# Sums over keys in a cross attention: one moving column against the weights, or ones as weights in four column groups with a block transpose on VectorE

## The chip, the core and the metric

The kernel runs on one core of a Trainium2 chip. The time is device microseconds of one execution. A core has TensorE (PE; its weight loads are shown apart, as PEld), VectorE (DVE), ScalarE (ACT), GpSimd (POOL) and the queues that start DMAs (SP among them). Matrix products go from SBUF through TensorE into PSUM, which has banks of 512 float32 columns in 128 partitions.

## What is computed

A decoder of two layers, float32, batch 4, 256 tokens of 256 features. The first layer has a self attention of 16 heads, a cross attention over 1601 context tokens and a feed-forward part with ternary weights. The second has a recurrence, a cross attention (the one changed here), and a mixture of eight experts. Cut to what matters, the second cross attention is, for each batch `b` and each of its 16 heads of width 128, in four groups that share keys and values:

```
q = rope(rmsnorm(LN(x) @ Wq))                  # 256 queries a head
k = rope(rmsnorm(concat(LN(x), ctx) @ Wk))     # 256 + 1601 = 1857 keys, one set for 4 heads
v = concat(LN(x), ctx) @ Wv
e = exp(q @ k.T / sqrt(128) - max)             # softmax over the keys
x = x + ((e @ v) / sum(e, over keys)) @ Wo
```

The kernel scales by folding factors into the keys, so the form is the same. The changed lines compute `1 / sum(e, over keys)`.

## The kernel before

The first part of the run, to about 560 us, takes the four batches through the first layer and the recurrence. From there to the end the second cross attention and the experts run interleaved.

The attention goes by pairs of heads (class `Pair`, 32 pairs: 4 batches, 4 groups, 2 pairs each). A pair has 2 x 256 = 512 queries, which are the free dimension of all its tiles; keys lie on the partitions, in 15 chunks of 128 (the last has 65). A pair passes through these stages:

- `score` (L1309): two score tiles bsc a step on TensorE (128 keys x 512 queries). ScalarE copies each to SBUF with the key's factor (L1310), VectorE keeps a running maximum acc (L1312, L1314).
- `maximum`: four transposes of acc (tm, L1321), a maximum on VectorE (mq, L1323), and four transposes that spread it over the partitions (bc, L1327).
- `exponential`: VectorE subtracts (L1331), ScalarE takes the exponential (L1334), and GpSimd adds the chunks up into one tile `sum` of 128 x 512 (L1337, L1346). Of the very last pair, VectorE adds the last chunks into a second tile `rest` (L1340, L1343).
- `weigh` (L1355): values times exponentials, summed over the chunks in one PSUM bank, bpo.
- `finish`: ScalarE copies bpo to aT (L1361). What is left in `sum` is the sum over 128 partitions, for each of the 512 queries. Line 1368 takes it: for each block of 128 queries a matmul with that block of `sum` as the stationary weights and one column of ones as the moving operand, which leaves the sums with the queries on partitions, one column for a block (ts, 128 x 4). VectorE takes the reciprocal (rs, L1373). Then aT is projected with the output weights (bpw, L1381, two matmuls for a head), and VectorE multiplies by rs and adds into x (L1385).

A matmul of float32 is carried out in two passes and each pass is a record of its own in the profile; each pass has its weight load.

Between the stages stand the preparations of the next group: projections and rotations of keys (pk, L1238; ropek, L1156; tpk, L1249; kTb, L1251) and queries (pq, L1199; ropeq; rnq, L1159; L1163; tpq, L1211), and the experts of the batch before (mph, L1013; it, L1018 to L1020; mpe, L1026; x, L1031). GpSimd adds the two halves of a rotation (L1156) and takes the power for the norm (L1159) in the same queue in which it sums the exponentials.

The order around the change is written out by hand: `steps` has one step for two key chunks, `put` gives the pieces of other work places between them, and a pair's `finish` is cut in four pieces by its yields, so that the sums, the two halves of the projection and the additions lie some steps apart. A scheduler then may move an instruction past neighbours on its engine. PSUM tiles such as bsc, tm, ts, pk and bpw come in turn from a ring of six banks (`p1`); a bank comes free when its last reader is done. Tiles of `sm` are small SBUF tiles with a given number of buffers.

Of the kernel before, what the change touches and what calls it, by code (L numbers as in the profile page):

```python
# [20 lines left out]
P = 128  # L21
# [94 lines left out]
def decoder_kernel(ctx: ExitStack, tc: tile.TileContext, at, t, out):  # L116
    nc = tc.nc
    V, A, G, T = nc.vector, nc.scalar, nc.gpsimd, nc.tensor
# [18 lines left out]
    def p1(name):  # L137

        ring[0] += 1
        if psb and ring[0] % 3 == 0:  # L140
            return psb[0].tile([P, 512], F32, tag="one", name=name, bufs=2)
        return psa.tile([P, 512], F32, tag="one", name=name, bufs=4)
# [17 lines left out]
    def fa(b, name, dt=F32):  # L160

        return fr.tile([P, 512], dt, tag=f"a{b}", name=name, bufs=NA)
# [9 lines left out]
    def sm(shape, tag, name, bufs=2, dt=F32):  # L172
        return small.tile(shape, dt, tag=tag, name=name, bufs=bufs)
# [30 lines left out]
    def cc(name):  # L204
        o, n = at[name]
        return cst[:, o : o + n]
# [1078 lines left out]
    class Pair:  # L1285
# [71 lines left out]
        def finish(self):  # L1357
            b, g, nm = self.b, self.g, self.nm
            e, su = gt[b, g], self.sum
            aT = fa(1, f"aT{nm}")  # L1360
            A.copy(aT, self.po)  # L1361
            yield

            ts = p1(f"ts{nm}")
            parts = (su, self.rest) if self.final else (su,)
            for i in range(4):
                for a in parts:
                    T.matmul(
                        ts[:, i : i + 1], lhsT=a[:, i * P : (i + 1) * P], rhs=cc("ones")[:, 0:1],
                        start=a is parts[0], stop=a is parts[-1],  # L1370
                    )
            rs = sm([P, 4], "rs", f"rs{nm}")
            V.reciprocal(rs, ts[:, 0:4])  # L1373
            if not self.final:
                yield

            for h in range(2):
                pw = p1(f"bpw{nm}{h}")
                for j in range(2):
                    o = h * 256 + j * P  # L1380
                    T.matmul(  # L1381
                        pw[:, j * 256 : j * 256 + 256], lhsT=aT[:, o : o + P], rhs=e["wo"][:, self.h + h, :], start=True, stop=True
                    )
                for j in range(2):
                    V.scalar_tensor_tensor(  # L1385
                        xs[b][:, j, :], pw[:, j * 256 : j * 256 + 256], rs[:, 2 * h + j : 2 * h + j + 1], xs[b][:, j, :], ALU.mult, ALU.add
                    )
                if not self.final:
                    yield
# [222 lines left out]
```

## Time and profile before

| what | value |
|---|---|
| time, median of 3 runs | 1772.86 us (1772.27 to 1773.15) |
| profiled execution, its own time | 1771.45 us |
| its span, first to last instruction | 1769.6 us |
| mean granted TensorE clock | 0.988 |
| sums (ts, L1368): matmul passes / weight loads | 264 / 264 |
| reciprocals (rs, L1373) | 32, median 173 ns |
| GpSimd adding into `sum` (L1346) | 411, 533.4 us |

A row of a group names line, engine, operation, output and inputs, their sizes, then the count and the durations. Durations of matmuls overlap, since TensorE starts a pass before the last one has left; the distance from start to start tells what a pass costs. In the chain of work that ended last each piece is what held up the next one; an engine that is not on it had time to spare there. The numbers around a duration in a wait name the instruction that ended it.

### The profile page before, as it was taken

To read this page: it belongs to the slowest core of one execution; us is meant where nothing else is said; L and a number is where in the kernel's file an instruction comes from. 1 tells how busy PE (TensorE), PEld (TensorE's weight loads), DVE (VectorE), ACT (ScalarE), POOL (GpSimd) and SP (SyncE) were. 2 spreads that over 40 slices of the span, in tenths; PEclk is the share of its full clock that TensorE was granted. 3 is DMA by queue.
4 is the path that set the end of the run, shared out by engine and by line. 5 is a ranking of instruction groups with operands and counts; after the bars stand their busy time and mean duration, and the time that the engine had idled before them with its cause. 6 is when DMAs were issued, how large, how long until landed. Compare 5 with 4: busy or idle time off the path is not lost.

```text
span 1769.6 us, 20922 instructions
## 1 busy us (share of the span) xinstructions
PE 1712.0 (97%) x6792; PEld 1017.1 (57%) x6792; DVE 1299.4 (73%) x2420; ACT 994.3 (56%) x1741; POOL 866.6 (49%) x719
## 2 busy tenths in 40 slices
PE   7989989988999999999999999999999999999998
PEld 4555668765555555455555656555565555555557
DVE  5662476789658777797787788788778778777775
ACT  2456653655556656567565555656555556655551
POOL 2210023212116677666776565676666656666460
PEclk9999999999999999999999999999999999999999
DMA  6321234201231011121211212121121203111102
GB/s 235 106 94 54 86 100 128 72 1 59 69 122 57 28 60 51 37 80 36 60 41 60 70 42 81 48 88 41 60 55 57 75 31 111 31 51 46 54 1 66
DMA packets 106565, 116.91 MB, mean 66 GB/s; under 512 B 9664, under 2 KB 80468, under 8 KB 106456
## 3 DMA queue, kind: packets, MB, share of 16 engines
q1 hardware_dynamic: 105160, 114.02, 20.9%
q10 hardware_dynamic: 1296, 1.54, 0.3%
q8 instruction: 55, 0.90, 0.2%
q14 instruction: 54, 0.44, 0.1%
HBM read 101.38 MB, written 14.16 MB: 65 GB/s over the span
## 4 chain that ended last, share of the span: by engine, by line
PE 75%; DVE 8%; ACT 7%; POOL 6%; issue 2%; DMA 1%; ACTq 0%; POOLq 0%; DVEq 0%
PE bpo L1355 19%; PE bsc L1309 19%; PE pk L1238 7%; PE vah L347 4%; POOL sum L1346 3%; PE bpw L1381 3%; PE mph L1013 3%; ACT s L1334 2%; PE pq L1199 2%; PE xsc L655 2%; ACT s L1310 2%; PE xpo L700 1%; PE mpe L1026 1%; PE sc L536 1%; PE tpk L1249 1%
## 5 line engine op out<-in xcount | busy, mean ns | idle before, releaser
L1346 POOL TENSOR_TENSOR sum<-sum,s 128x512 f32<-128x512 f32 (+1 forms) x411 | 533.4, 1298 | 84.8 <-ACT s L1334 59.0
L1309 PE MATMUL bsc<-qTb,kTb 128*128 128x512 f32 (+1 forms) x960 | 457.7, 597 | 2.4 <-ACT kTb L1251 2.3
L1355 PE MATMUL bpo<-s,vb 128*128 128x512 f32 (+1 forms) x960 | 458.7, 596 | 0.0
L1310 ACT ACTIVATE s<-bsc,kn 128x512 f32<-128x512 f32 (+1 forms) x480 | 317.4, 684 | 232.8 <-PE bsc L1309 217.8
L1314 DVE SCALAR_TENSOR_TENSOR acc<-bsc,kn,acc 128x512 f32<-128x512 f32 x448 | 333.8, 745 | 104.0 <-ACT s L1310 89.3
L1331 DVE TENSOR_TENSOR s<-s,bc 128x1024 f32<-128x1024 f32 (+1 forms) x256 | 289.5, 1143 | 15.2 <-PE bc L1327 15.1
L1334 ACT ACTIVATE s<-s 128x1024 f32<-128x1024 f32 (+1 forms) x256 | 256.4, 1006 | 52.3 <-DVE s L1331 50.7
L1309 PEld LDWEIGHTS bsc<-qTb,kTb 128*128 128x128 f32 (+1 forms) x960 | 174.2, 187 | 186.5 <-issue 135.2
L1355 PEld LDWEIGHTS bpo<-s,vb 128*128 128x128 f32 (+1 forms) x960 | 169.1, 191 | 131.9 <-issue 129.6
L1156 POOL TENSOR_TENSOR ropek<-ropek,ropuk 128x512 f32<-128x512 f32 (+1 forms) x64 | 77.0, 1203 | 182.3 <-DVE ropuk L1151 181.3
L1337 POOL TENSOR_TENSOR sum<-s 128x512 f32<-128x512 f32 x32 | 40.9, 1277 | 187.1 <-ACT s L1334 187.1
L1238 PEld LDWEIGHTS pk<-wkv,cTk 128*128 128x128 f32 x832 | 101.6, 192 | 9.2 <-issue 4.5
L1163 ACT ACTIVATE ropeq<-ropeq,rnq 128x128 f32<-128x128 f32 x128 | 41.2, 390 | 112.6 <-POOL rnq L1159 109.0
L1238 PE MATMUL pk<-wkv,cTk 128*128 128x128 f32 x832 | 103.3, 275 | 0.0
L347 PE MATMUL vah<-wv,vcT 128*128 128x512 f32 (+1 forms) x156 | 80.0, 651 | 4.9 <-DMA vcT<-in_ctxT 2.9
L1312 DVE TENSOR_SCALAR acc<-bsc,kn 128x512 f32<-128x512 f32 x32 | 24.0, 750 | 64.2 <-ACT s L1310 64.2
L1381 PEld LDWEIGHTS bpw<-wo,aT 128*128 128x128 f32 x256 | 49.7, 194 | 34.7 <-issue 23.0
L1159 POOL TENSOR_TENSOR kn<-ssk,nhalf 128x4 f32<-128x4 f32 (+1 forms) x64 | 64.9, 1015 | 8.9 <-DVE ssk L1158 8.9
L1156 POOL TENSOR_TENSOR ropeq<-ropeq,ropuq 128x512 f32<-128x512 f32 x32 | 43.8, 1369 | 47.5 <-ACT s L1310 35.5
L1381 PE MATMUL bpw<-wo,aT 128*128 128x256 f32 x256 | 67.0, 386 | 0.0
L350 ACT COPY vst<-vah 128x512 f32<-128x512 f32 (+1 forms) x52 | 30.3, 590 | 63.0 <-PE vah L347 30.2
L268 POOL TENSOR_TENSOR rsr_xa<-rse_xa,nhalf 128x2 f32<-128x2 f32 x4 | 3.4, 853 | 126.0 <-DVE rse_xa L266 126.0
(500 smaller groups left out, 2592.2 us busy)
## 6 DMA issues: line engine op xcount, KB each, us to landing
cTk<-in_ctxT SPq DMA_DIRECT2D x32, 512.0 KB
v<-vst SPq DMA_DIRECT2D x48, 256.0 KB
vb<-v SPq DMA_DIRECT2D x48, 256.0 KB
wq<-in_wq SPq DMA_DIRECT2D x16, 512.0 KB
wo<-in_wo SPq DMA_DIRECT2D x16, 512.0 KB
wi<-in_wi SPq DMA_DIRECT2D x32, 256.0 KB
vcT<-in_ctxT SPq DMA_DIRECT2D x12, 512.0 KB
xcT<-in_ctxT SPq DMA_DIRECT2D x12, 512.0 KB
```

What stands on the lines that cost most here:

```text
L347: T.matmul(pv[0:r, :], lhsT=cT[:, c, k * P : k * P + r], rhs=wv[c], start=c == 0, stop=c == 1)
L1156: G.tensor_tensor(r4, r4, u4[:, :, ::-1, :], ALU.add)
L1159: G.tensor_tensor(rn, ss[:, 0:n], nhalf[:, 0:n], ALU.pow)
L1238: T.matmul(pk[:, q, 0:w], lhsT=src, rhs=e["wkv"][:, c, 0:w], start=c == 0, stop=c == 1)
L1309: T.matmul(pc[0:n, :], lhsT=e["kT"][:, k * P : k * P + n], rhs=q, start=True, stop=True)
L1310: A.activation(s[0:n, i, :], pc[0:n, :], AF.Copy, scale=e["kn"][0:n, k : k + 1])
L1314: V.scalar_tensor_tensor(self.acc[0:n, :], pc[0:n, :], e["kn"][0:n, k : k + 1], self.acc[0:n, :], ALU.mult, ALU.max)
L1331: V.tensor_tensor(s[0:n, 0:w, :], s[0:n, 0:w, :], self.bc[0:n, None, :].to_broadcast([n, w, 512]), ALU.subtract)
L1334: A.activation(s[0:n, 0:w, :], s[0:n, 0:w, :], AF.Exp)
L1346: G.tensor_tensor(self.sum[0:n, :], self.sum[0:n, :], s[0:n, i, :], ALU.add)
L1355: T.matmul(self.po, lhsT=e["v"][0:n, k, :], rhs=self.s[c][0:n, i, :], start=k == 0, stop=k == NCH - 1)
L1381: T.matmul(pw[:, j * 256 : j * 256 + 256], lhsT=aT[:, o : o + P], rhs=e["wo"][:, self.h + h, :], start=True, stop=True)
```

## The change

The four matmuls of a pair's sums change sides. Before, a block of `sum` (128 x 128) is the weights and one column of ones moves. After, 32 columns of ones are the weights, and 128 columns of `sum` move: query number 32 i to 32 i + 31 of each of the four blocks, so the moving operand is read in four runs of 32 columns. Matmul i writes the 32 PSUM partitions from 32 i; all 32 hold the same sums, for 128 queries. VectorE transposes the 128 x 128 result in blocks of 32 x 32 into a new SBUF tile `sq` with one buffer, after which the sum of query 128 k + p stands in partition p, column 32 k. The reciprocal reads these four columns from SBUF. For the last pair, the two parts are now the outer loop: four matmuls of `sum`, then four of `rest`.

```diff
             ts = p1(f"ts{nm}")
             parts = (su, self.rest) if self.final else (su,)
-            for i in range(4):
-                for a in parts:
+            for a in parts:
+                for i in range(4):
                     T.matmul(
-                        ts[:, i : i + 1], lhsT=a[:, i * P : (i + 1) * P], rhs=cc("ones")[:, 0:1],
+                        ts[32 * i : 32 * i + 32, 0:P], lhsT=cc("ones")[:, 0:32],
+                        rhs=a.rearrange("p (k q) -> p k q", k=4)[:, :, 32 * i : 32 * i + 32],
                         start=a is parts[0], stop=a is parts[-1],
                     )
+            sq = sm([P, P], "sq", f"sq{nm}", 1)
+            V.transpose(sq, ts[:, 0:P])
             rs = sm([P, 4], "rs", f"rs{nm}")
-            V.reciprocal(rs, ts[:, 0:4])
+            V.reciprocal(rs, sq.rearrange("p (k q) -> p k q", k=4)[:, :, 0])
```

In the built programs TensorE, GpSimd and the DMA queues keep the order of their instructions, apart from one bpo matmul in one place and, in the last pair, one of two matmuls of mph that follow the sums, which stands behind the projection bpw instead of ahead of it. On VectorE a transpose stands where each reciprocal stood, and the reciprocal comes, in most pairs, one instruction later. A few instructions of VectorE and ScalarE that prepare the angles of a batch or take exponentials change places with neighbours.

## The prediction

> **What bounds the kernel now.** I read the page's first part, then the chain that ended last, then the groups of the line that is changed.
>
> ```profile
> PE 1712.0 (97%) x6792; PEld 1017.1 (57%) x6792; DVE 1299.4 (73%) x2420; ACT 994.3 (56%) x1741; POOL 866.6 (49%) x719
> PE 75%; DVE 8%; ACT 7%; POOL 6%; issue 2%; DMA 1%; ACTq 0%; POOLq 0%; DVEq 0%
> L1368 PEld LDWEIGHTS ts<-cst,sum x256: 188/192/193, 580.2 to 1729.6; 128*128 128x128 f32 x128
> L1368 PE MATMUL ts<-cst,sum x256: 166/250/251, 580.7 to 1729.7; 128*128 128x1 f32 x128
> L1373 DVE RECIPROCAL rs<-ts x32: 161/173/183, 586.2 to 1730.2; 128x4 f32<-128x4 f32 x32
> ```
>
> TensorE is busy for 97% of the span and carries 75% of the chain, so time taken out of its stream counts where the chain runs through that stream. The sums (L1368) are 128 matmuls with one moving column each, plus 8 more for the last pair's `rest`; every one is split in two passes (256 and 16 records), and each pass loads its own 128x128 weights. Stretched out in time for TensorE, one group of sums looks like this (start, duration of the whole group, number of passes):
>
> ```profile
> 579.80 1.02 PE L1309 MATMUL bsc<-qTb,kTb 128*128 128x512 f32 x2
> 580.66 0.95 PE L1368 MATMUL ts<-cst,sum 128*128 128x1 f32 x8
> 581.47 1.96 PE L1355 MATMUL bpo<-s,vb 128*128 128x512 f32 x4
> 583.27 0.59 PE L1309 MATMUL bsc<-qTb,kTb 128*128 128x512 f32 x1
> ```
>
> A pass of 512 columns takes 0.43 us of the stream: the two scores (bsc) start at 579.80 and the sums at 580.66. The eight passes of the sums hold the stream until 581.47, 0.81 us, or 0.10 us each, for one column apiece. The four bpo passes then need 583.27 - 581.47 = 1.80 us, where four times 0.43 is 1.72: the second bpo weight load was queued behind the sums' loads. One group of sums therefore costs 0.81 + 0.08 = 0.89 us, and all single groups stand between the same kind of neighbours and repeat this to some hundredths.
>
> **The change, on TensorE.** It removes the eight passes that each load 128 weight columns and puts in four matmuls (eight passes) with 32 weight columns and 128 moving columns, each into its own 32 output partitions. The trace before has this form: the self attention weighs its values (L571, L574) in four groups of 32 columns. One such place, TensorE alone:
>
> ```profile
> 97.39 1.98 PE L347 MATMUL vah<-wv,vcT 128*128 128x512 f32 x4 [0.63 <-ACT pT L557]
> 99.30 0.64 PE L571 MATMUL po<-pT,values 128*32 128x256 f32 x8
> 99.76 0.40 PE L574 MATMUL po<-sm,values 128*32 128x128 f32 x8
> 100.09 1.78 PE L446 MATMUL pq<-wqkv,xqkv 128*128 128x256 f32 x7
> ```
>
> L571's eight passes of 256 columns hold the stream for 99.76 - 99.30 = 0.46 us. At 0.43/512 us a column one pass is 0.215, so eight in a row would be 1.72 us: four run at once, in two sets. L574's passes, which have the 128 columns of the new ones, go from 99.76 to 100.09, 0.33 us: two sets of 0.11 are 0.22, and 0.11 more lies ahead of the next matmul of full width. Ahead of 99.30 the last of the four vah passes ended at about 97.39 + 4 x 0.43 = 99.11 to 99.2 (the first was late by its weights), a gap of 0.09. Sum of the new group: 0.09 to get into the narrow form, 0.03 for the first narrow weights (L571's first set takes 0.46 - 0.215 = 0.245), 2 x 0.11 for the sets, 0.11 to get out, and 0.11 for the next 128 weight columns, which can't be loaded ahead: 0.56 us. Against 0.89 one group saves 0.33 us.
>
> The last pair has two parts: 16 passes before, 1728.30 to 1730.01 = 1.71 plus 0.08; after, four sets instead of two, 0.56 + 0.22 = 0.78. It saves 1.0. The order of the built instructions also moves one of two matmuls of mph (L1013) there from ahead of bpw to behind it: bpw comes 0.43 sooner, and mph has slack, since the products (`it`) wait on VectorE anyway.
>
> A rule speaks against this. The Trainium skill, page "TensorEngine Tiling (Array Packing)", section "Instruction Overhead", gives a matmul a floor of about 60 cycles, so one moving column costs as much as 60; the page "TensorE: Matmul & The Clock Gate" puts the floor at about 25 ns. By that rule eight passes would be 0.2 us, the new group 0.36 us dearer, and the kernel about 20 x 0.36 = 7 us slower. The row decides: 0.10 us a pass, because each pass brings 128 new weight columns. I take the row.
>
> **What of it lies on the path.** The chain in order of time passes through a sum group in some pairs and beside it in others. Two stretches (start, us):
>
> ```profile
> 614.59 1.72 PE bsc L1309 x4
> 616.31 0.79 PE ts L1368 x8
> 617.10 1.82 PE bpo L1355 x4
> ...
> 580.42 1.23 POOL sum L1346
> 581.64 0.98 POOL rnq L1159
> 582.62 0.02 issue
> 582.65 1.28 ACT ropeq L1163 x4
> ...
> 588.11 0.33 ACT kTb L1251
> 588.44 0.04 issue
> 588.48 1.98 PE bsc L1309 x4
> ```
>
> At 616 the chain runs through the sums. At 580 it runs through GpSimd (rotation of q behind queued sums) and ScalarE, and TensorE waits at 588.48 whatever it did at 580.66: a faster group only makes that wait longer. Read through the whole chain, the groups at 616, 689, 767, 804, 839, 913, 993, 1076, 1117, 1155, 1230, 1309, 1350, 1389, 1469, 1543, 1622, 1662, 1694 and 1713 are on it, 20 in all, and the last double one; eleven are not. So 20 x 0.33 = 6.6, plus 1.0 + 0.43 at the end: 8.0 us. The eleven are costed at nothing: POOL and ACT hide them, and they would give 3.6 us more if that work came earlier too. Some of the 20 must have a second path close behind; I take off 1.0 us (three groups), an estimate.
>
> **The clock at the end.** The profile by windows (length, then busy time and count of PE, PEld, DVE, ACT, POOL, granted clock, DMA):
>
> ```profile
> 1727.20:1730.60 3.40, 3.40 (x22) 2.63 (x22) 1.20 (x2) 0.58 (x1) 0.47 (x1) 1.00 0.02 5
> 1730.60:1734.00 3.40, 3.40 (x10) 2.65 (x9) 0.79 (x2) 0.00 (x0) 0.00 (x0) 0.51 0.00 0
> ```
>
> Right behind the last sums the clock is 0.51, and the eight bpw passes start 0.43 us apart, where 0.215 is the pace of 256 columns. Seven gaps of 0.21 are 1.5 us on the chain. The two other half-clock stretches among the pairs (from 754 and 1062) follow waits of TensorE of 2.3 us and more, so I read this one as an answer to 1.7 us of one-column passes. With 0.8 us of full passes I expect it to go: 1.5 us, at worst nothing.
>
> **VectorE.** It gains 32 transposes of 128x128 from PSUM. No such row exists; the nearest, a product of 128x128 from PSUM (L1150), takes 0.28 us on average, the reciprocal of four columns 0.173. I take 0.28, with ends of 0.17 and 0.6 (should it run at half that pace). The reciprocal stays at 0.16 to 0.18. That is 32 x 0.28 = 9.0 us of VectorE, on an engine that is busy for 914 of the 1168 us from 560 to 1728. The transpose inherits the reciprocal's wait for the sums and its place; one other instruction stands between it and the reciprocal. Queued behind it are the running maxima (acc L1314) that free score buffers. In the place shown, the sums end at 581.6 and the reciprocal runs at 586.20, so the wait is long over, and its first user (x L1385) runs at 591.23. I cost it at nothing; idle time of VectorE hides it. Without that cover it is 21 x 0.28 = 5.9 us. GpSimd and the DMA queues keep their order; ScalarE moves a few instructions by two or three places.
>
> **Sum.** 8.0 - 1.0 + 1.5 = 8.5 us off the profiled execution's own 1771.45 us (span 1769.6 and 1.85 around it), 1762.95. The median of the runs shown is 1772.86, 1.4 above that execution; the same saving gives **1764.4**.
>
> **Rivals.**
> *Everything passes through* (chance 0.10). The eleven also give 3.6, nothing is taken off: 8.0 + 3.6 + 1.5 = 13.1, 1759.8. For it: what GpSimd waits for begins with TensorE's own scores. Against: those scores lie ahead of the sums in each of the eleven.
> *The gain is absorbed* (0.12). GpSimd's sums or VectorE's transposes become the late part in most pairs. VectorE at full price takes 5.9 of 8.5 and leaves 2.6: 1770.3, no measurable change. For it: 0.28 us against 0.33 saved, pair by pair; the waits for mq at 753, 1062 and 1376 come when VectorE or ScalarE is late. Against: 254 us of idle VectorE in that stretch.
> *The four groups don't run at once* (0.08): slower. The new moving operand is read in four runs of 32 columns, while L571's and L574's is contiguous; no row shows such a read. In series, eight passes of 0.11 make the group 0.09 + 0.03 + 0.88 + 0.11 + 0.11 = 1.22, 0.33 dearer than now; 20 x 0.33 + 0.3 = 6.9 slower, 1779.8. It decides from where a set of four takes over 0.275 us instead of 0.11.
>
> **How the numbers follow.** The forecast has 0.70, with its own range of 1761 to 1768 (clock and second paths either way). The range for 8 in 10 reaches to the case where everything passes and toward the absorbed one: 1759.5 to 1769.3. Under 0.2%, 3.5 us, no change can be told from none: faster 0.80, same 0.12, slower 0.08.
>
> **What would show it.** Right: the sums' passes start in sets of four, 0.11 us apart, and the stream is held 0.45 us, with 0.11 more at the next pass; the wait at 588 grows by 0.3; the half clock at 1730 is gone; transposes near 0.28 us with the reciprocal still long ahead of x. Wrong: narrow passes 0.1 us apart one by one; new waits of bsc or bc on DVE; VectorE's chain share up by more than 0.3 points.

## The result and the profile after

The changed kernel takes 1764.06 us (median of 6 runs, 1762.96 to 1767.17), the kernel before 1772.26 beside it (6 runs): a ratio of 0.9958, interval 0.9945 to 0.997. By the ratio it is faster by 0.42%, 7.4 us (the medians lie 8.2 apart). The forecast was 1764.4.

The page of the profile after, busy time and the chain:

```profile
PE 1697.8 (96%) x6792; PEld 986.5 (56%) x6792; DVE 1301.3 (74%) x2452; ACT 994.5 (56%) x1741; POOL 867.1 (49%) x719
PE 71%; DVE 9%; ACT 8%; POOL 7%; issue 3%; DMA 1%; POOLq 0%; ACTq 0%; DVEq 0%
```

TensorE is busy for 14 us less and the span is 7.1 shorter (1762.5 against 1769.6). From the first to the last sums it is busy for 9.6 us less (1128.3 against 1137.9) and the time is 4.5 shorter: about half of what TensorE saved stayed as time in which it waits. The groups of the sums, and one of them in time, TensorE alone:

```profile
L1369 PEld LDWEIGHTS ts<-sum,cst x256: 106/108/110, 581.1 to 1724.3; 128*32 128x32 f32 x128
L1369 PE MATMUL ts<-sum,cst x256: 272/285/298, 581.1 to 1724.4; 128*32 128x128 f32 x128
L1375 DVE STREAM_TRANSPOSE sq<-ts x32: 300/305/318, 586.5 to 1724.9; 128x128 f32<-128x128 f32 x32
L1377 DVE RECIPROCAL rs<-sq x32: 159/162/178, 587.4 to 1725.3; 128x4 f32<-128x4 f32 x32
```
```profile
580.14 1.02 PE L1309 MATMUL bsc<-qTb,kTb 128*128 128x512 f32 x2
581.10 0.42 PE L1369 MATMUL ts<-sum,cst 128*32 128x128 f32 x8
581.45 1.98 PE L1355 MATMUL bpo<-s,vb 128*128 128x512 f32 x4
583.27 1.02 PE L1309 MATMUL bsc<-qTb,kTb 128*128 128x512 f32 x2
```

From the start of the two scores to the first score behind bpo there are now 583.27 - 580.14 = 3.13 us, of which six passes of 0.428 are 2.57: the sums cost 0.56. In the kernel before it was 583.27 - 579.80 = 3.47, so 0.90. Taken from single starts, a group costs 0.559 us in 30 of the 32 pairs, against 0.899 before: 0.34 less in each.

For a reading by place I laid the start of each pair's sums beside the same start before. The stretch up to the first sums has no edit in it and differs by itself (0.43 us later here, between 1.7 earlier and 1.5 later in the other profiles). From the first to the last sums the time goes from 1147.64 to 1143.13 us, 4.51 less; from the last sums to the end (the tail) from 41.33 to 38.32, 3.01 less. Between two groups the time changes by -0.34 or by nothing, nearly in turn. Two pairs lose: pair 6 0.96, pair 12 0.29. The windows behind the last sums, with the columns of the prediction, have no half clock:

```profile
1723.20:1726.60 3.40, 3.40 (x27) 2.19 (x26) 1.67 (x4) 0.59 (x1) 0.43 (x1) 1.00 0.02 5
1726.60:1730.00 3.40, 2.02 (x10) 1.43 (x9) 3.24 (x11) 0.38 (x1) 0.00 (x0) 1.00 0.09 24
```

### The profile page after: what moved, and what is told of

It is laid out like the page before. It is cut to its first block, busy times and chain, and to the rows that moved or that the text cites. A ratio compares the mean times of both kernels' runs of the same rounds, so it can differ in the third digit from the quotient of the medians.

```text
span 1762.5 us, 20956 instructions
## 1 busy us (share of the span) xinstructions
PE 1697.8 (96%) x6792; PEld 986.5 (56%) x6792; DVE 1301.3 (74%) x2452; ACT 994.5 (56%) x1741; POOL 867.1 (49%) x719
## 4 chain that ended last, share of the span: by engine, by line
PE 71%; DVE 9%; ACT 8%; POOL 7%; issue 3%; DMA 1%; POOLq 0%; ACTq 0%; DVEq 0%
PE bpo L1355 18%; PE bsc L1309 18%; PE pk L1238 7%; POOL sum L1346 4%; PE vah L347 4%; PE mph L1013 3%; PE bpw L1385 3%; ACT s L1334 2%; ACT s L1310 2%; PE pq L1199 2%; PE xpo L700 1%; PE sc L536 1%; PE xsc L655 1%; PE mpe L1026 1%; POOL ropeq L1156 1%
## 5 line engine op out<-in xcount | busy, mean ns | idle before, releaser
L1334 ACT ACTIVATE s<-s 128x1024 f32<-128x1024 f32 (+1 forms) x256 | 256.5, 1006 | 54.9 <-DVE s L1331 53.4
L1149 ACT ACTIVATE squares<-pk 128x256 f32<-128x256 f32 (+1 forms) x128 | 46.9, 372 | 33.9 <-PE pk L1238 30.2
```

The lines of the kernel that those rows point to most:

```text
L1334: A.activation(s[0:n, 0:w, :], s[0:n, 0:w, :], AF.Exp)
```

## The experiments

A build is scheduled anew, so an edit can move instructions elsewhere; where it did so and it matters, it is said. The edits are shown shortened; n is the number of a pair, 0 to 31. Ratios are to the kernel before, run beside the experiment.

**The eleven pairs beside the chain, alone.**

```diff
+            new = n in (0, 2, 4, 8, 10, 12, 16, 18, 22, 24, 26)
+            if new:      # four column groups, transpose
+            else:        # as before
```

> The new sums in the eleven pairs whose group lay beside the chain (0, 2, 4, 8, 10, 12, 16, 18, 22, 24, 26), the old form in all others. Theory (GpSimd and ScalarE set the time there): each group is 0.34 us shorter on TensorE, the next wait is 0.34 us longer, and the stretch from the first to the last sums stays within 0.5 us of 1147.6; time 1771.5 to 1773. Rival (TensorE's time counts everywhere): 11 x 0.34 = 3.7 us less, about 1768.5.

Measured: 1771.27 us, ratio 0.9998, interval 0.9989 to 1.0007; between the sums 1147.27 us (-0.37), tail 41.33. The groups are short and the time stays. TensorE at the first of these pairs, this run and then the kernel before (start, duration, wait before it):

```profile
588.86 1.55 PE L1309 MATMUL bsc<-qTb,kTb 128*128 128x512 f32 x3 [0.76 <-ACT kTb L1251]
```
```profile
588.48 1.98 PE L1309 MATMUL bsc<-qTb,kTb 128*128 128x512 f32 x4 [0.42 <-ACT kTb L1251]
```

The wait for the copy of kT is 0.76 us instead of 0.42: the 0.34 saved are waited for again, eight microseconds later. (The whole run starts its first sums 0.47 later, so the start itself is later too.) Of the 0.37 us, 0.29 come in one stretch, from pair 20 to 21, both of which keep the old sums here: TensorE's waits there are shorter in this build, and the chain of this run no longer passes through pair 20's sums.

**The twenty pairs on the chain, alone.**

```diff
+            new = n in (1, 3, 5, 6, 7, 9, 11, 13, 14, 15, 17, 19, 20, 21, 23, 25, 27, 28, 29, 30)
```

> The new sums in the twenty pairs whose group lay on the chain, the old form in the eleven others and in the last pair. Theory: 17 of the 20 pay 0.34 us (5.8), pair 6 loses about 1 us to the exponential that stands ahead of the copy of kT on ScalarE in this build too, so the stretch from the first to the last sums is 4.3 to 5.1 us shorter, the tail stays at 41.3; time 1767 to 1768. Rival (gain spread evenly over the pairs): 20/31 of 4.5, 2.9 us less.

Measured: ratio 0.9964 (0.9951 to 0.9978), 1764.33 us. Between the sums 1143.11 us, 4.53 less, in the predicted span. The eleven others give nothing: apart from pair 20's stretch, the two runs split the gain of 4.5 us cleanly. The tail, which was to stay at 41.3, took 39.65 with the same instructions; that is the half clock, of which below. The time itself is 3 us under what was expected: in the profile 1.7 of that is the tail, and 1.7 lies ahead of the first sums, where nothing is edited.

**The last pair alone.**

```diff
+            new = self.final
```

> The new sums in the very last pair alone. Theory: the stretch between the sums is unchanged, and the tail from the last sums to the end goes from 41.3 to 38.3 us with no half clock behind the sums; time about 1769.3. Rival (the half clock came from where its time windows fell, not from the one-column passes): the half clock stays or comes elsewhere, and the tail is only 1.0 to 1.5 us shorter.

Measured: 1768.77 us, ratio 0.9985 (0.9976 to 0.9993); between the sums 1147.73, as before; tail 38.32, with no half clock. The theory holds on the size, not yet on the cause.

**All but the last pair, and the kernel before once more.** Both keep the old sums at the end.

```diff
+            new = not self.final
```

> The whole change except in the very last pair, which keeps the old sums. Theory: the stretch between the sums is 4.5 us shorter as in the changed kernel; the tail is 39.7 us without a half clock and 41.3 with one, against 38.3 with the new form. The half clock, if it is caused by the one-column passes alone, must come (41.3); if it also depends on where the clock's time windows fall, it may be away (39.7).

> The kernel before once more, for the half clock behind the last sums. If the one-column passes alone bring it, the tail is 41.3 us again; if it depends on where the time windows fall as well, it may be 39.7.

Measured: the first 1766.54 us, ratio 0.9969 (0.9957 to 0.9981), between the sums 1143.04, tail 39.64; the second, one run of 1773.11 us, tail 39.66. The windows around the last sums in the kernel before, run again (same columns as in the prediction), and its TensorE behind them:

```profile
1730.60:1734.00 3.40, 3.40 (x22) 2.65 (x21) 1.16 (x2) 0.59 (x1) 0.43 (x1) 1.00 0.02 5
1734.00:1737.40 3.40, 3.08 (x15) 2.37 (x13) 2.01 (x6) 0.28 (x1) 0.00 (x0) 1.00 0.00 0
```
```profile
1734.33 1.89 PE L1381 MATMUL bpw<-wo,aT 128*128 128x256 f32 x8
1736.05 1.03 PE L1013 MATMUL mph<-yTm,wi 128*128 128x256 f32 x4
```

The clock is 1.00 and the eight bpw passes take 1.72 us from start to next start, although the same one-column passes ran just ahead. Of five profiles with the old sums at the end, two (the first one of before, and the eleven pairs) have the half clock and a tail of 41.33; three have none and 39.65. Of the eight profiles with the new form at the end (the changed kernel and seven experiments), none has it, and the tail is 38.31 to 38.32. So the new form itself is worth 39.65 - 38.32 = 1.33 us at the end, and the half clock 1.68, where it comes.

The profiles also show where the clock's steps fall. In each profile every half-clock stretch begins a whole number of 3.413 us after the first one (in the kernel before, 754.4, 1061.6 and 1730.6 are 90 and 196 such steps apart). In the two profiles with the half clock the last sums begin 1.1 and 0.8 us into a step; in the three without, 0.1, 0.2 and 3.0 us. The new form in the last pair alone began 1.1 us into a step and had none. That would fit if the place in the step and the form both have a part, but these few profiles don't show it.

**The order on ScalarE kept.** In pair 6's stretch the changed kernel waits as the one before doesn't. ScalarE and TensorE there, after and then before:

```profile
809.14 0.67 ACT L1310 ACTIVATE s<-bsc,kn 128x512 f32<-128x512 f32 x1
809.71 1.05 ACT L1334 ACTIVATE s<-s 128x1024 f32<-128x1024 f32 x1
810.66 0.68 ACT L1310 ACTIVATE s<-bsc,kn 128x512 f32<-128x512 f32 x1
811.23 0.42 ACT L1251 COPY kTb<-tpk 128x321 f32<-128x321 f32 x1
...
811.71 1.55 PE L1309 MATMUL bsc<-qTb,kTb 128*128 128x512 f32 x3 [1.23 <-ACT kTb L1251]
```
```profile
809.85 1.25 ACT L1310 ACTIVATE s<-bsc,kn 128x512 f32<-128x512 f32 x2
810.99 0.43 ACT L1251 COPY kTb<-tpk 128x321 f32<-128x321 f32 x1
811.29 1.08 ACT L1334 ACTIVATE s<-s 128x1024 f32<-128x1024 f32 x1
...
811.47 1.98 PE L1309 MATMUL bsc<-qTb,kTb 128*128 128x512 f32 x4
```

An exponential of 1.05 us (L1334) moved ahead of the copy of kT. One ordering edge undoes it (`keep_behind` holds the exponential behind that copy in ScalarE's order; no other engine's order changes):

```diff
         A.copy(e["kT"][:, 512 * i : 512 * i + w], tp[:, 0:w])
+        kt_last[b, g, i] = latest()[0][mybir.EngineType.Activation]
...
+            here = latest()[1]
             A.activation(s[0:n, 0:w, :], s[0:n, 0:w, :], AF.Exp)
+            if (self.b, self.g, self.h, c) == (0, 3, 2, 5):
+                keep_behind(({mybir.EngineType.Activation: kt_last[1, 0, 3]}, here))
```

> The whole change, and one ordering edge that keeps an exponential of pair 7 behind the last copy of kT of the group after it on ScalarE, as in the kernel before. Theory: the wait of 1.2 us of bsc for kT at 811 shrinks to under 0.5, pair 6 costs at most 0 instead of 0.96 us: about 1 us under the changed kernel. Rival (the wait comes from the transpose, or from TensorE being early): the wait stays over 1 us and the time is that of the changed kernel.

Measured: 1763.51 us, ratio 0.9954 (0.9941 to 0.9966). The same place in this run:

```profile
807.77 1.25 ACT L1313 ACTIVATE s<-bsc,kn 128x512 f32<-128x512 f32 x2
808.91 0.43 ACT L1253 COPY kTb<-tpk 128x321 f32<-128x321 f32 x1
809.21 2.03 ACT L1338 ACTIVATE s<-s 128x1024 f32<-128x1024 f32 x2
...
809.39 1.98 PE L1312 MATMUL bsc<-qTb,kTb 128*128 128x512 f32 x4 [0.28 <-ACT kTb L1253]
```

The wait is 0.28 instead of 1.23 and pair 6 costs 0.00 instead of 0.96 us: the moved exponential is the cause. The medians of the two kernels, 0.5 us apart with single runs spread over 2.7 and 4.2 us, can't show 1 us; the profiles do. Between the sums this run takes 1141.66. That is 1.47 less than the changed kernel; the half microsecond beyond pair 6 is the clock: neither half-clock stretch (754, 1062) came in this profile. And the first of them turned out to cost nothing: without it, TensorE reached 784 earlier by 1.2 us and waited there 1.0 us for kT behind three 1 us angle functions on ScalarE. Pairs 4 and 5 together come out 0.36 earlier, in the changed kernel 0.38.

**Column groups one after the other.** All four matmuls write the same 32 partitions; the last pair is as changed, and rs is the reciprocal of ones, so the division by the sums is left out; the transpose takes these 32 partitions.

```diff
-                        ts[32 * i : 32 * i + 32, 0:P], lhsT=cc("ones")[:, 0:32],
+                        ts[0:32, i * P : (i + 1) * P], lhsT=cc("ones")[:, 0:32],
...
-            V.reciprocal(rs, sq.rearrange("p (k q) -> p k q", k=4)[:, :, 0])
+            V.reciprocal(rs, cc("ones")[:, 0:4])
```

> As changed, but all four matmuls of a pair's sums (not of the last pair) write the same 32 output partitions, so they use one column group; rs is the reciprocal of ones and the division by the sums is left out. Theory (four column groups run at once): in one group the passes follow each other 0.11 us apart, a group costs about 1.2 us instead of 0.56, and the kernel is slower than before: 1772 + 20 x 0.3 - 3 = about 1775. Rival (the saving comes from the 32-column weight load alone): a group stays near 0.56 us and the time near 1764.

Measured: 1802.47 us, ratio 1.0178 (1.0163 to 1.0194). One group:

```profile
579.56 1.06 PE L1369 MATMUL ts<-sum,cst 128*32 128x128 f32 x8
580.55 1.98 PE L1355 MATMUL bpo<-s,vb 128*128 128x512 f32 x4
582.37 0.59 PE L1309 MATMUL bsc<-qTb,kTb 128*128 128x512 f32 x1
```

A group holds the stream for 0.99 us and costs 1.194, 0.30 more than before; the passes start 0.11 us apart. So it is the four groups at once that pay, not the short weight load. The sixteen pairs that pay in the changed kernel (all odd ones to 29, and 28) each show +0.29 to +0.30. The whole, though, is 27 us worse than the 1775 expected: without the sums in rs's way, VectorE and ScalarE have another order in some 60 places each, and between the sums waits for kT of up to 2 us stand. What of the 27 us comes from which is not settled; the run decides on the group alone.

**A contiguous moving operand.**

```diff
-                        rhs=a.rearrange("p (k q) -> p k q", k=4)[:, :, 32 * i : 32 * i + 32],
+                        rhs=a[:, i * P : (i + 1) * P],
```

> As changed, with the moving operand read as 128 columns in a row instead of four runs of 32 (the sums come out for the queries in another order). Theory (the runs cost nothing): the group holds 0.559 us of the stream as in the changed kernel. Rival (runs cost something): a set of four starts less than 0.11 us after the other, the group is shorter by 0.02 us or more.

The sums belong to other queries here. No other instruction moved. Measured: one run, 1764.57 us, between the sums 1143.15 against 1143.13. The group:

```profile
581.23 0.43 PE L1369 MATMUL ts<-sum,cst 128*32 128x128 f32 x8
581.59 1.98 PE L1355 MATMUL bpo<-s,vb 128*128 128x512 f32 x4
```

It holds the stream for 0.36 us, as in the changed kernel (0.35): four runs of 32 columns cost nothing.

**Three transposes.**

```diff
+            for _ in range(3):
                 V.transpose(sq, ts[:, 0:P])
```

> As changed, with the transpose carried out three times. Theory (idle VectorE hides it): 0.61 us more of VectorE a pair, and under 2 us more in all, from moved instructions. Rival (VectorE is on the path where the sums are): 20 x 0.61 = 12 us more, about 1776.

Measured: 1771.86 us, ratio 1.0004 (0.9995 to 1.0013): about 8 us over the changed kernel, between what the two expected. It isn't spread. In 28 of the 31 distances between sums the change is as in the changed kernel or better; the stretches from pairs 4, 12 and 20 are 4.2, 3.5 and 2.6 us longer than before. TensorE's waits for the maximum in that part (us in all, times, longest), after and then with three transposes:

```profile
PE bc L1327 <- DVE mq L1323: 5.9, 3, 2.8
```
```profile
PE bc L1327 <- DVE mq L1323: 11.7, 3, 4.9
```

These waits are not VectorE at work. GpSimd at pair 4's place, the scaling of q on ScalarE that waits for it, and the first score that VectorE then takes, after and then with three transposes:

```profile
747.71 1.26 POOL L1156 TENSOR_TENSOR ropeq<-ropeq,ropuq 128x512 f32<-128x512 f32 x1
748.93 1.01 POOL L1159 TENSOR_TENSOR rnq<-ssq,nhalf 128x4 f32<-128x4 f32 x1
749.92 1.26 POOL L1346 TENSOR_TENSOR sum<-sum,s 65x512 f32<-65x512 f32 x1
...
749.97 1.28 ACT L1163 ACTIVATE ropeq<-ropeq,rnq 128x128 f32<-128x128 f32 x4 [6.07 <-POOL rnq L1159]
...
751.86 0.75 DVE L1312 TENSOR_SCALAR acc<-bsc,kn 128x512 f32<-128x512 f32 x1 [5.24 <-ACT s L1310]
```
```profile
749.00 1.27 POOL L1156 TENSOR_TENSOR ropeq<-ropeq,ropuq 128x512 f32<-128x512 f32 x1
750.23 1.26 POOL L1346 TENSOR_TENSOR sum<-sum,s 65x512 f32<-65x512 f32 x1
751.45 1.01 POOL L1159 TENSOR_TENSOR rnq<-ssq,nhalf 128x4 f32<-128x4 f32 x1
...
752.49 0.98 ACT L1163 ACTIVATE ropeq<-ropeq,rnq 128x128 f32<-128x128 f32 x3 [8.63 <-POOL rnq L1159]
...
754.08 0.75 DVE L1312 TENSOR_SCALAR acc<-bsc,kn 128x512 f32<-128x512 f32 x1 [7.51 <-ACT s L1310]
```

VectorE stands idle for 7.51 us ahead of this score, behind which the maximum mq stands in its queue: it waits for ScalarE, which waits for GpSimd's rnq. In this build GpSimd takes one sum of 1.26 us ahead of rnq where the changed kernel takes it behind, at these three places and for no other rnq of the 32. At pair 4's place rnq starts 2.52 us later: 1.26 is that sum, the rest came with GpSimd's queue, which began its sums later. Half clock behind the longer waits (6.8 us of it twice, where the changed kernel has 3.4, and 3.4 at 1381, where it has none) adds to them. VectorE and ScalarE have another order in some 80 and 70 places too, so what the transposes' own time adds at these three places is not shown.

**Sums by transposes on TensorE.** Not a part of the change; another way to the same sums, in all pairs but the last:

```diff
+                for i in range(4):
+                    T.transpose(ts[:, i * P : (i + 1) * P], su[:, i * P : (i + 1) * P], ident)
+                V.tensor_reduce(rs, ts.rearrange("p (i k) -> p i k", i=4), AX.X, ALU.add)
+                V.reciprocal(rs, rs)
```

> Another way to the sums, in all pairs but the last: four transposes on TensorE of the 128 x 512 sums into PSUM and an addition over the free dimension on VectorE. Four transposes hold the stream 0.44 us (tm, L1321), so a group costs 0.12 us less than 0.56; VectorE has 0.68 + 0.17 us instead of 0.31 + 0.16. Theory: 17 groups pay, 2 us under the changed kernel, about 1762, if VectorE's longer work is hidden too. Rival (VectorE's 0.38 us more a pair counts): 17 x 0.38 - 2 = 4.5 us over it.

Measured: 1773.26 us, ratio 1.0009 (1.0 to 1.0017).

```profile
L1382 DVE TENSOR_REDUCE rs<-ts x31: 672/681/693, 587.3 to 1721.3; 128x4 f32<-128x512 f32 x31
```

The pairs that paid 0.34 pay 0.45 to 0.46 here, as expected. The stretches from pairs 4, 12 and 20 lose 3.85, 3.55 and 3.55 us, the same three places. At all three GpSimd again takes a sum ahead of rnq, as with three transposes and in no other run. Neither theory had it; how much of the 11 us VectorE's longer work costs by itself is not shown.

**The two ways mixed,** with the ordering edge: TensorE's transposes in the sixteen pairs that pay, column groups elsewhere.

> The change with the ordering edge of the run before, and in the sixteen pairs that were seen to pay (1, 3, 5, 7, 9, 11, 13, 15, 17, 19, 21, 23, 25, 27, 28, 29) the sums by four transposes on TensorE and an addition on VectorE instead of four column groups. Theory (VectorE's longer work costs only in pairs 4, 6, 12 and 20, which stay as changed): a group of the sixteen saves 0.45 us instead of 0.34, 1.8 us in all, so the stretch between the first and last sums is 7 to 8 us shorter than the 1147.6 of before and the time 1.5 to 2 us under the change with the edge. Rival (moved instructions eat it): within 1 us of that run.

Measured: 1765.06 us, ratio 0.9959 (0.9945 to 0.9972), not better. Two neighbouring pairs gain 0.44 together in place of 0.34, but the wait for kT behind the angle functions, at 786 here, grew from 1.0 to 2.2 us, with 3.4 us of half clock behind it: the stretch from pair 5 is 3.7 us longer, the one ahead of it 1.3 shorter. Pair 12's is 1.5 longer, with 6.8 us of half clock at 1062. Between the sums 1144.88, 2.8 less than before where 7 to 8 were expected. The rival holds: by the ratios the run lies 0.9 us above the one with the edge. The change with the edge (1763.51) stays the fastest seen, by less than its runs can tell from the change alone.

## Why the prediction was right

*The bound and the group.* Right to the second digit: 0.56 against 0.89 forecast, 0.559 against 0.899 measured; the rows of the self attention carried over, and the serial form came to 1.19 where its rival had 1.22. The rule of the Trainium skill ("TensorEngine Tiling (Array Packing)", section "Instruction Overhead"), by which one column costs as much as 60 and the change would have lost, was rightly set aside for the row: eight passes hold the stream for 0.81 us, not 0.2, and in the trace of before their weight loads start 0.11 us apart, as the passes do. One count was wrong without harm: the last pair's `rest` has 4 matmuls and 8 passes, not 8 and 16; the sum took the 16 passes of the whole last group from their starts.

*Which groups pay.* All eleven that the chain passes by gave nothing, alone (0.9998) and in the whole. Of the twenty on the chain 17 have a shorter stretch; pairs 6, 14 and 30 don't (at 30 the projection bpw now waits 0.32 us for the copy aT, which takes back the group's saving; at 14 it goes in small gaps ahead of the next transposes tpk and tpq). Pair 20's 0.27 is not its group's: with the old sums, in the run of the eleven, its stretch is 0.29 shorter too. So sixteen are shown to pay, and the forecast's 17, with three groups taken off as an estimate, was off by one.

*The step that was wrong inside a right sum* is "ScalarE moves a few instructions by two or three places", costed at nothing. One of these moves costs 0.95 us, as the ordering edge shows, so pair 6 didn't merely fail to pay. With this and pair 12's 0.29, which lies within what the half clock at 1062 does by itself (the kernel before, run again, is 1.64 us longer there), the pairs gave 4.5 us instead of 5.6.

*The tail.* 1.43 us forecast for the last sums and the moved mph, 1.33 measured. The half clock was read as an answer to the one-column passes. That is too simple: three of five profiles with these passes have none. The saving of 1.5 us (1.68 measured) is there only in some executions with the old sums. The profiles account for 4.5 + 1.3 us, and 0.7 (two in five of 1.68) is an estimate of the half clock's share: 6.5, where the ratio says 7.4 with an interval of 5 to 10. That the time came within 0.4 us of the forecast is partly luck: the forecast took 8.5 us, all of the half clock among them, from a median of 1772.86 that came out as 1772.26 over six runs.

*VectorE.* 0.305 us a transpose, 0.28 forecast. That idle time hides one is right: sixteen pairs pay the whole 0.34 us that TensorE saves with the transpose in each, the waits for mq stayed (5.9 us after, 6.1 before), and even three transposes cost nothing in 28 of 31 places. What a transpose costs without that cover, 5.9 us in the prediction, no run shows: in the two runs with more work on VectorE, three stretches grew by up to 4.2 us, but there GpSimd had changed its order, which it keeps in the changed kernel. One sign of being wrong did come, VectorE's share of the chain, from 8% to 9%. It was no use as a sign: the kernel before, run again, has 9% too.

## What to carry to other kernels

Here a matmul pass with one moving column took as long as its weight load: both start 0.11 us apart, for 128 weight columns. With ones as narrow weights and the data moving in four column groups the same sums took 0.56 instead of 0.90 us, with the 0.10 us ahead of the first narrow pass and the 0.10 us more of the full passes behind included. Before summing such savings, go through the chain in order of time and count only the instances that it passes through; here that was 20 of 31, sixteen of which paid, and of the other eleven ten changed the time by 0.03 us at most. And compare the instruction order of the two builds on every engine, ahead of any account of a surprise: an edit on TensorE moved one exponential on ScalarE and lost three pairs' worth, and one on VectorE moved three sums on GpSimd.

## What was not expected of the hardware

Half-clock stretches come in some executions and not in others, at the same place of the work. In the two profiles of the kernel before, the one behind the last sums came once, and the one at 1062 took 3.4 and 6.8 us; the run with the ordering edge had none among the pairs. One stretch of 3.4 us cost 1.7 us behind the last sums, and nothing at 754, where the time without it was waited for kT.

At 754 the steps of 3.41 us seem to decide. Ten profiles have a wait of 2.3 us for mq there: in the eight in which 2.04 us or more of it fell into one step, the half clock followed; in the two in which 1.97 and 1.71 did (the ordering edge and the mixed form), none came. So the prediction's reading, that waits of 2.3 us and more bring it, leaves out how the steps cut a wait. That is seen in these profiles, not tested by an edit. How much of the spread of single runs (1769.6 to 1774.3 us for the kernel before) they make was not worked out, and why some last sums bring one and others don't was not found.
